# A new opening, maxima 42 items ahead and transposed a half later, and row sums inverted once on 128 partitions

## The chip, the core and the metric

The kernel runs on one core of a Trainium2 chip. The time is the device time of one execution in microseconds (us); three timed executions of the kernel before gave 4222.73 to 4227.74 us, with a median of 4225.1 us. The profile is of one more execution. The engines are PE (TensorE, matmuls), DVE (VectorE), ACT (ScalarE), POOL (GpSimd) and SP (SyncE, which only issues DMAs here).

## What is computed

The input x is 4 batches of 2048 tokens of 512 numbers, all in float32. It is normalized per token (layernorm without weights), and two things are added to x: attention with 16 heads of 32, whose queries and keys pass a filter in the frequency domain, and a layer of 8 experts that sends each token to the best one, at most 100 tokens to each.

```
xn = layernorm(x)
q, k, v = split(xn @ w_qkv)                       # 16 heads of 32
q, k = irfft(rfft(q) * mask), irfft(rfft(k) * mask)   # along the 32 of a head
out = softmax(q @ k.T / sqrt(32)) @ v             # 2048 x 2048 scores a head and batch
x + out @ w_out + b_out + experts(xn)
```

The filter is linear in a head's 32 numbers, so the kernel applies it once to the columns of w_qkv and not to q and k.

## The kernel before

**Tiles and loops.** Four heads are worked on together (HG = 4), so there are B * NG = 16 groups k of a batch and four heads, and each has NQ = 4 blocks of 512 queries: 64 blocks. A block goes over the 2048 keys in NT = 16 key tiles of 128. One key tile of a block is a *half*; two of them are a *window*. There are 1024 halves. In a half PE makes the scores of 128 keys by 512 queries for four heads (`scores`), ACT takes the exponentials into a tile `even` or `odd`, and PE multiplies the tile of the half before with v (`products`), which DVE adds up in `num`.

**Maxima.** The softmax subtracts each query's maximum, which must be known before a block's scores are made. So the scores are also made a first time, the other way round (queries on partitions), and DVE reduces them (`max_matmuls`, `max_reduce`, into `part`). An item of `stream` is 128 queries by 512 keys for two heads; 32 items make a block, and each half holds two items. The first MAX_AHEAD = 40 items are done in the opening, so a block's last item falls in half 11 of the block before the one before it is needed, 20 halves ahead. There DVE makes `neg` (`max_negate`), and at the end of the same half, or inside a projection of that half, PE transposes it (`max_turn`). ACT copies it (`max_store`), and at the head of the next window POOL splits it in three bfloat16 parts, which three SP DMAs `negm<-row` bring to four partitions (`max_split`). At a block's start PE puts them into the scores' banks (`shift`). After the first scores of a block, keys are held as differences of neighbours (`steps_of_keys`, by POOL), so that scores add up in PSUM from one key tile to the next.

**Row sums.** The exponentials of a block are added up pairwise: POOL issues a DMA that adds the odd tile to the even one (`even<-odd`, 1 MB, one a window), and POOL adds the result to that of the window before. Five halves into the next block PE sums the last tile over its 128 keys with a matrix of ones, and the four heads' sums stand on 32 equal partitions each (`close_steps`, `fold`; ACT copies them to `den`). DVE inverts `den` in eight pieces of 128x64, one a half in halves 6 to 13 (`invert`, into `factor`). At the head of half 14 POOL multiplies `num` with `factor` (`divide`, into `ot`). In halves 17 to 20 PE multiplies `ot` with w_out (`result`), and in half 21 POOL issues a DMA that adds the 1 MB to the output (`out_dram<-y`). The last block but one (of the 63 that are closed so) has other places, and the last block its own function.

**Order.** All engines work in the order in which the instructions are written out (`InOrder`). What is not the main line of a half is put into `agenda[half]` by `plan`: projections for the next group (pieces of 128 tokens, cost 1 each), token tiles of the next batch, the routing, loads. `spread` lays the pieces out so that PE's costs are even; key pieces may not come before a half that depends on MAX_AHEAD (`SPENT`), as the keys of the group are still needed by maxima. SP too issues in program order, but runs ahead of the others where a DMA has nothing to wait for.

**Opening.** SP loads the query and key columns of w_qkv (2 MB), the first batch of x (4 MB), and copies value columns. All four groups' weights are filtered (`filter_steps`: `turned` transposes on PE and copies on DVE, `filtered` multiplies on PE and copies on ACT), group 0's into `wg`, the others' through `wd` in DRAM. Then tokens are measured (DVE), scaled (POOL), normalized and transposed (`turn`). Projections of the first keys and queries go over 512 tokens at once. The first 40 items of maxima follow, one at a time, with turns and projections put in at written-out places (`ahead`).

Most instructions are issued by the helper in line 84 (`InOrder`), so that line says little in the profile; the names of tiles say more.

Of the kernel before, what the change touches and what calls it, by code (L numbers as in the profile page):

```python
# [39 lines left out]
PART = 64  # L40
WIN = 2
NW = NT // WIN
MAX_AHEAD = 40
# [3 lines left out]
def shape_constants():  # L47

    d = np.arange(DH)
    angle = 2.0 * np.pi * np.outer(np.arange(NF), d) / DH  # L50
    waves = np.concatenate([np.cos(angle), np.sin(angle)])

    waves[[NF, 2 * NF - 1]] = 0.0
    weight = np.full(NF, 2.0 / DH)
    weight[[0, NF - 1]] = 1.0 / DH
    weighted = waves * np.concatenate([weight, weight])[:, None]
    freq = np.stack([np.tile(weighted, (1, P // DH)), np.tile(waves, (1, P // DH))], axis=1)
    i = np.arange(P)
    eye = np.eye(P)
    upto = i[:, None] <= i[None, :]  # L60
    same_head = i[:, None] // DH == i[None, :] // DH
    square = np.stack([eye, upto, same_head], axis=1)
    falling = np.broadcast_to(E - np.arange(E), (P, E))
    token = np.arange(NT)[None, :] * P + i[:, None]
    return {
        "c_freq": freq.astype(np.float32),
        "c_square": square.astype(np.float32),
        "c_falling": np.ascontiguousarray(falling, dtype=np.float32),
        "c_token": token.astype(np.float32),
    }  # L70
# [33 lines left out]
def attention_and_top1_experts(ctx: ExitStack, tc: tile.TileContext, a: dict, out: bass.AP):  # L104
# [28 lines left out]

    mask = const.tile([2 * NF, 1], F32, name="mask")
# [5 lines left out]
    square = const.tile([P, 3, P], F32, name="square")  # L140
    nc.scalar.dma_start(out=square, in_=a["c_square"])
    ident, upto, same_head = (square[:, j, :] for j in range(3))
# [30 lines left out]
    wd = [dram1.tile([P, NR, 3, P], F32, name=f"wd{c}") for c in range(NG)]  # L173
    wg = {}
    raw = {}
    for s in range(2):
        both = probs(s == 1)
        for g in range(NR // 2):
            raw[s, g] = both[:, g]
            nc.sync.dma_start(out=raw[s, g], in_=w_qkv[:, 2 * g : 2 * g + 2, s * DM : (s + 1) * DM])  # L180
# [14 lines left out]
    def filter_steps(c):  # L195

        held = {}

        def turned(s):
            if s == 0:  # L200
                held["wt"] = probs(c % 2 == 1)
            pt = bank()
            for r in range(NR):
                on.tensor.transpose(
                    pt[:, r * P : (r + 1) * P], raw[s, r // 2][:, r % 2, c * P : (c + 1) * P], ident
                )
            on.vector.tensor_copy(held["wt"][:, s, 0, :], pt)

        def filtered(s):
            pw = bank()  # L210
            wt = held["wt"][:, s]
            for r in range(NR):
                at = slice(r * P, (r + 1) * P)
                on.tensor.matmul(pw[:, at], lhsT=wt[:, 0, at], rhs=filt, start=True, stop=True)
            done = pw.rearrange("p (r n) -> p r n", r=NR)
            if c == 0:
                on.scalar.copy(wg[0, s], done)
            else:
                on.scalar.copy(wt[:, 1, :], pw)
                nc.sync.dma_start(out=wd[c][:, :, s, :], in_=wt[:, 1, :].rearrange("p (r n) -> p r n", r=NR))  # L220

        return [lambda f=f, s=s: f(s) for s in range(2) for f in (turned, filtered)]
# [7 lines left out]
    def token_stage(b):  # L230
# [10 lines left out]
        def load_tile(i):  # L241
            n, t = divmod(i, TQ)
            if t == 0:
                held[n] = chunk("xs")
            on.sync.dma_start(out=held[n][:, t : t + 1, :], in_=x[b, n, :, t : t + 1, :])
# [163 lines left out]
    def load_qkv_weights(k, s):  # L409
        wg[k, s] = weights.tile([P, NR, P], F32, name=f"w{s}", bufs=1)  # L410
        on.sync.dma_start(out=wg[k, s], in_=wd[k % NG][:, :, s, :])
# [294 lines left out]
    def close_steps(k, n):  # L706
# [12 lines left out]

        def divide():  # L720
            held["ot"] = work.tile([P, QB], F32, tag="ot", name="ot", bufs=1)
            on.gpsimd.tensor_tensor(held["ot"], ended[k, n][0], held["factor"], ALU.mult)
# [15 lines left out]
        else:  # L738
            steps = [(5, 1, fold)] + [(6 + i, 0, invert, i) for i in range(QB // PART)]
# [20 lines left out]
    load, measure, scale, normalize, turn, first_route, first_sums, _ = token_stage(0)  # L760

    load(0)
# [3 lines left out]
    for s in range(3):  # L766
        wg[0, s] = weights.tile([P, NR, P], F32, name=f"w{s}", bufs=1)
    nc.sync.dma_start(out=wg[0, 2], in_=w_qkv[:, :, 2 * DM : 2 * DM + P])
    for c in range(1, NG):
        cols = slice(2 * DM + c * P, 2 * DM + (c + 1) * P)  # L770
        nc.sync.dma_start(out=wd[c][:, :, 2, :], in_=w_qkv[:, :, cols])
    filters = [filter_steps(c) for c in range(NG)]
    turned, filtered = ([f[2 * s + i] for f in filters for s in range(2)] for i in range(2))
    for i in range(2 * NG + 1):
        if i < 2 * NG:
            turned[i]()
        if i > 0:
            filtered[i - 1]()
        if 2 * NG - TQ <= i < 2 * NG:
            measure(i - 2 * NG + TQ)  # L780
    for s in range(3):
        nc.sync.dma_start(out=wd[0][:, :, s, :], in_=wg[0, s])
    first_projections = projections(0, TQ)
# [4 lines left out]
    for i in range(TQ):  # L788
        measure(TQ + i)
    scale(TQ, 2 * TQ, on.vector)  # L790
    for i in range(TQ, 2 * TQ):
        normalize(i)
        measure(TQ + i)
    first_projections[0]()
    scale(2 * TQ, 3 * TQ, on.vector)
    for i in range(2 * TQ, 3 * TQ):
        if i == 3 * TQ - 1:
            first_projections[1]()
        normalize(i)
        measure(TQ + i)  # L800
    scale(3 * TQ, NT, on.vector)
    falling = const.tile([P, E], F32, name="falling")
    nc.scalar.dma_start(out=falling, in_=a["c_falling"])
    token = const.tile([P, NT], F32, name="token")
    nc.scalar.dma_start(out=token, in_=a["c_token"])

    w_gate = const.tile([P, NR, DH], F32, name="w_gate")
    nc.gpsimd.memset(w_gate, 0.0)
    nc.scalar.dma_start(out=w_gate[:, :, 0:E], in_=a["L0_ffn_w_gate"].rearrange("(r p) e -> p r e", p=P))
    b_out = const.tile([P, DM], F32, name="b_out")  # L810
    nc.scalar.dma_start(out=b_out, in_=a["L0_attn_b_out"].partition_broadcast(P))


# [5 lines left out]
    for table in tables:  # L819
        nc.sync.dma_start(out=table.rearrange("(t p) c -> p t c", p=P), in_=nobody)  # L820

    load_out_weights(0)

    ahead = {6: first_projections[2], 14: first_projections[3], 22: first_projections[4]}
    ahead.update({28: first_projections[5], 33: first_projections[6]})
    for i, item in ((4, 1), (8, 9), (12, 17)):
        ahead.update({item + 2 * j: lambda i=i + 2 * j: (turn(i), turn(i + 1)) for j in range(2)})
    ahead.update({4: lambda: normalize(12), 5: lambda: normalize(13)})
    ahead.update({7: lambda: normalize(14), 8: lambda: normalize(15)})
    first_projections = projections(0)[7 * TQ :]  # L830
    on.sync = InOrder(tc, nc.sync)
    key_steps(0)
    closing = {}
    for i, item in enumerate(stream[:MAX_AHEAD]):
        if i == 30:
# [3 lines left out]
        half = next(turns), next(turns)  # L839
        max_matmuls(item, half)  # L840
        max_reduce(item, half, False)
        if i in ahead:
            ahead[i]()
        if i in (7, 15, 23):
            key_steps((i + 1) // 8)
        while full_blocks:
            closing[i + 2] = full_blocks.pop(0)
            max_negate(*closing[i + 2])
        if i in closing:
            negated.append(closing[i])  # L850
            max_store(max_turn(bank(), 0))
            max_split(*closing[i])
# [35 lines left out]
    def spread(steps, last):  # L888
# [4 lines left out]
        def places(level):  # L893
            half, done, found = base, costs[base], []
            for cost, first, _ in steps:
                while half < first or done + cost / 2 > level * (half - base + 1):
# [48 lines left out]
    def plan(k):  # L945
# [4 lines left out]
        def after_keys_are_spent():  # L950

            for i, place in enumerate([j for j, s in enumerate(kinds) if s == 1]):
                cost, _, step = steps[place]
                steps[place] = cost, start + SPENT + i // TQ * TQ, step

# [7 lines left out]
        steps, kinds = [], []  # L963
        if k == 0:
            done = spread([(1, 0, step) for step in first_projections], 15)
# [18 lines left out]
        if c == NG - 1:  # L984
# [14 lines left out]
            done = spread(steps, last)  # L999
# [6 lines left out]
        else:  # L1006
            steps = [(1, ready if k == 0 else start, step) for step in pieces]
            after_keys_are_spent()
            done = spread(steps, last)
# [37 lines left out]
    pairs, adds, splits = {}, {}, {}  # L1047
    left = None
    window = 0
    maxima = stream[MAX_AHEAD:]  # L1050
    for k in range(B * NG):
        for n in range(NQ):
            num = work.tile([P, QB], F32, tag="num", name="num")
            tiles = {}
            for w in range(NW):
# [9 lines left out]
                for j in (even, odd):  # L1065
# [16 lines left out]
                    while full_blocks:  # L1082
                        splits[window + 1] = full_blocks.pop(0)
                        max_negate(*splits[window + 1])
                        negated.append(splits[window + 1])
# [58 lines left out]
```

## Time and profile before

| | |
|---|---|
| median of three timed executions | 4225.1 us (4222.73 to 4227.74) |
| the profiled execution | 4220.07 us |
| its span, from the first to the last instruction | 4218.3 us |
| PE / DVE / ACT / POOL busy in it | 99% / 82% / 59% / 70% |
| mean granted clock of PE | 0.998 |
| first scores matmul (end of the opening) | 99.5 us |
| DMA engines' time taken by POOL's queue / SP's queue | 73.5% / 5.4% |

Busy shares are of the span. The chain is followed back from the last instruction, each time to what released it; its shares say on which engine the end depended. A group's line has the engine, the operation, output and inputs by name, the shape, the count, then busy us and the mean duration in ns, then the idle time of the engine just before. A line of the order of time has its start and duration in us, a count of merged instructions, and in brackets the idle time before it and what ended it. Weight loads (PEld) lie beside the matmuls. Matmuls are pipelined: the distance from start to start says more than a duration.

### The profile page before, as it was taken

How to read it: one execution, taken by the hardware profiler on the slowest of the kernel's cores; microseconds unless marked ns; L12 is line 12 of the kernel's file. 1: busy time of each engine (PE TensorE's matmuls, PEld its weight loads, DVE VectorE, ACT ScalarE, POOL GpSimd, SP SyncE). 2: the span in 40 equal slices, each digit the busy share in tenths (PEclk: the TensorE clock that was granted, in tenths of full speed). 3: DMA queues.
4: the chain of work that ended last, by engine and by line, in shares of the span. 5: the costliest groups of instructions: out<-in, count | busy, mean ns of one | idle time of the engine just before them, and what ended most of it. 6: DMA issues, size and time to landing. Idle time of an engine off the chain costs nothing.

```text
span 4218.3 us, 120261 instructions
## 1 busy us (share of the span) xinstructions
PE 4166.4 (99%) x52270; PEld 1837.7 (44%) x52270; DVE 3440.0 (82%) x4962; ACT 2489.1 (59%) x3411; POOL 2968.4 (70%) x2046
## 2 busy tenths in 40 slices
PE   8999999999999999999999999999999999999998
PEld 4444444444444444444444444444444443444432
DVE  6778888987788888897788888888778888788896
ACT  3555556666565556657565556566656555556665
POOL 1567776776876767776687766767668776677873
PEclk9999999999999999999999999999999999999999
DMA  4667778997788778899677787899877976778788
GB/s 121 144 139 154 155 159 163 220 197 151 139 158 161 155 156 164 187 199 193 132 158 157 156 161 150 162 199 203 169 148 146 183 158 134 148 160 165 156 170 178
DMA packets 183416, 685.93 MB, mean 163 GB/s; under 512 B 26902, under 2 KB 56760, under 8 KB 117608
## 3 DMA queue, kind: packets, MB, share of 16 engines
q0 software_dynamic: 110432, 605.83, 73.5%
q1 hardware_dynamic: 71280, 71.90, 5.4%
q8 instruction: 409, 6.70, 0.6%
q14 instruction: 119, 0.97, 0.1%
q10 hardware_dynamic: 1176, 0.52, 0.1%
HBM read 71.85 MB, written 88.96 MB: 38 GB/s over the span
## 4 chain that ended last, share of the span: by engine, by line
PE 93%; DVE 5%; DMA 1%; issue 1%; ACT 0%; POOL 0%; SPq 0%; ACTq 0%; POOLq 0%; DVEq 0%
PE array L84 93%; DVE part L84 3%; DVE num L84 1%; DVE factor L84 0%; DMA even<-odd 0%; ACT odd L84 0%; DVE stats L84 0%; DMA w<-wd 0%; ACT even L84 0%; DMA odd<-in_L_attn_w_qkv_dram 0%; DVE even L84 0%; POOL rstd L84 0%; DVE neg L84 0%; DMA mask<-_L_attn_mask_logits_dram 0%; DVE mv L84 0%
## 5 line engine op out<-in xcount | busy, mean ns | idle before, releaser
L84 DVE TENSOR_REDUCE part<-array 128x1 f32<-128x512 f32 (+1 forms) x3132 | 2483.3, 848 | 681.0 <-PE array L84 678.0
L84 POOL TENSOR_TENSOR even<-even 128x1024 f32<-128x1024 f32 x876 | 2123.6, 2528 | 410.5 <-DMA even<-odd 406.5
L84 PE MATMUL array<-keys,q 32*128 32x512 f32 x8192 | 2066.0, 614 | 7.9 <-DVE num L84 2.9
L84 PE MATMUL array<-q,steps_of_keys 32*128 32x512 f32 x8192 | 2030.7, 616 | 2.4 <-issue 2.1
L84 ACT ACTIVATE odd<-array 128x1024 f32<-128x1024 f32 x1024 | 996.0, 1021 | 483.3 <-PE array L84 413.4
L84 ACT ACTIVATE even<-array 128x1024 f32<-128x1024 f32 x1024 | 994.2, 1021 | 447.6 <-PE array L84 434.8
L84 PEld LDWEIGHTS array<-keys,q 32*128 32x128 f32 x8192 | 776.9, 184 | 565.8 <-DVE part L84 351.1
L84 PEld LDWEIGHTS array<-q,steps_of_keys 32*128 32x128 f32 x8192 | 691.9, 184 | 274.6 <-issue 250.8
L84 POOL DMA_DIRECT2D even<-odd x510 | 464.8, 911 | 394.9 <-ACT odd L84 346.6
L84 DVE TENSOR_TENSOR num<-num,array 128x512 f32<-128x512 f32 x960 | 650.5, 678 | 23.5 <-PE array L84 23.4
L84 PEld LDWEIGHTS array<-xnT,w 128*32 128x32 f32 x15808 | 443.3, 110 | 264.0 <-DVE part L84 172.3
L84 PE MATMUL array<-even,v 128*32 128x512 f32 x4096 | 545.5, 605 | 1.0 <-DVE part L84 1.0
L84 PE MATMUL array<-odd,v 128*32 128x512 f32 x4096 | 545.9, 605 | 0.0
L84 PE MATMUL array<-xnT,w 128*32 128x128 f32 (+1 forms) x15808 | 525.2, 277 | 1.5 <-ACT xnT L84 0.7
L84 PEld LDWEIGHTS array<-w,xnT 128*32 128x32 f32 x8192 | 230.4, 110 | 146.8 <-DVE part L84 106.6
L84 DVE RECIPROCAL factor<-den 128x64 f32<-128x64 f32 x504 | 274.4, 545 | 0.0
L84 PE MATMUL array<-wo,ot 128*32 128x512 f32 x2048 | 267.0, 594 | 5.0 <-POOL ot L84 5.0
L84 PE MATMUL array<-w,xnT 128*32 128x128 f32 x8192 | 269.4, 273 | 1.3 <-DMA w<-wd 1.1
L84 PEld LDWEIGHTS array<-even,v 128*32 128x32 f32 x4096 | 80.6, 108 | 390.1 <-DVE part L84 381.2
L84 PEld LDWEIGHTS array<-odd,v 128*32 128x32 f32 x4096 | 80.8, 108 | 388.4 <-DVE part L84 379.9
L84 POOL DMA_DIRECT2D out_dram<-y x63 | 86.5, 1373 | 202.8 <-ACT y L84 125.6
L84 ACT COPY q<-array 128x128 f32<-128x128 f32 (+1 forms) x250 | 66.9, 268 | 186.1 <-PE array L84 182.3
(129 smaller groups left out, 1478.9 us busy)
## 6 DMA issues: line engine op xcount, KB each, us to landing
even<-odd POOLq DMA_DIRECT2D x510, 1024.0 KB, 8.4
out_dram<-y POOLq DMA_DIRECT2D x63, 1024.0 KB, 9.8
xs<-in_L_attn_x_dram SPq DMA_DIRECT2D x96, 256.0 KB
out_dram<-in_L_attn_x_dram SPq DMA_DIRECT2D x16, 1024.0 KB
w<-wd SPq DMA_DIRECT2D x45, 256.0 KB
wo<-in_L_attn_w_out_dram SPq DMA_DIRECT2D x16, 256.0 KB
negm<-row SPq DMA_DIRECT2D x192, 4.0 KB
xs<-in_L_attn_x_dram SPq DMA_DIRECT2D x2, 1024.0 KB
```

What stands on the lines that cost most here:

```text
L84: done = act(*args, **kwargs)
```

## The change

**Row sums.** For 62 of the 63 blocks, the eight reciprocals are replaced. In half 6 an SP DMA takes one partition of `den` for each head (4 x 512) and lays it out as 128 partitions of 16, in the first 16 columns of `factor` (`apart`). In half 9 DVE inverts these in place (`invert_all`). In half 10 an SP DMA writes them to DRAM (`lay_down`), and in half 12 four SP DMAs read each head's 512 numbers back onto 32 partitions (`to_rows`). The division stays at the head of half 14. The last block but one keeps its eight reciprocals.

**Maxima.** MAX_AHEAD is 42, so a block's last item falls in half 10. `max_negate` stays there, but the block is entered in `negated` only in the next half, so that PE transposes in half 11; `max_split` stays at the head of the next window.

**Opening.** The constant matrices come in one DMA on SP's queue, ahead of all. Of w_qkv the first 128 query and key columns are loaded first, then the first four token tiles in two DMAs, then the remaining columns and the rest of x. Group 0's weights are filtered first, group 1's around the first token tiles, groups 2 and 3 beside the maxima. Projections are pieces of 128 tokens throughout. 42 items of maxima are done in 21 pairs: the matmuls of both items, then both reductions, then the steps in `beside[p]`. Value weights are read from w_qkv directly and no longer copied to DRAM. The four tables are cleared by a DMA with a contiguous run for each partition, beside the last pairs.

**Plan.** `SPENT` follows MAX_AHEAD and comes one half earlier; `spread` is given the latest half of each key piece and does not pass it.

```diff
-MAX_AHEAD = 40
+MAX_AHEAD = 42
+APART = HG * QB // P
...
+    square = const.tile([P, 3 * P + E + NT], F32, name="square")
+    nc.sync.dma_start(out=square, in_=a["c_square"])
...
     for s in range(2):
-        both = probs(s == 1)
-        for g in range(NR // 2):
-            raw[s, g] = both[:, g]
-            nc.sync.dma_start(out=raw[s, g], in_=w_qkv[:, 2 * g : 2 * g + 2, s * DM : (s + 1) * DM])
+        raw[s] = probs(s == 1).rearrange("p g r n -> p (g r) n")
+        nc.sync.dma_start(out=raw[s][:, :, 0:P], in_=w_qkv[:, :, s * DM : s * DM + P])
...
+        def apart():
+            on.sync.dma_start(out=held["factor"][:, 0:APART], in_=held["den"][0::DH, :])
+
+        def invert_all():
+            at = held["factor"][:, 0:APART]
+            on.vector.reciprocal(at, at)
+
+        def lay_down():
+            held["all"] = scratch.tile([P, APART], F32, name="inverses")
+            on.sync.dma_start(out=held["all"], in_=held["factor"][:, 0:APART])
+
+        def to_rows():
+            for h in range(HG):
+                row = held["all"][DH * h : DH * (h + 1), :].rearrange("r c -> (r c)")
+                on.sync.dma_start(out=held["factor"][DH * h : DH * (h + 1), :], in_=row.partition_broadcast(DH))
...
-            steps = [(5, 1, fold)] + [(6 + i, 0, invert, i) for i in range(QB // PART)]
+            steps = [(5, 1, fold), (6, 0, apart), (9, 0, invert_all), (10, 0, lay_down), (12, 0, to_rows)]
             first = 17
...
+    for step in (*turned0, *filtered0):
+        step()
+    for i in range(TQ):
+        measure(i)
+    for step in turned1:
+        step()
     scale(0, TQ, on.vector)
     for i in range(TQ):
         normalize(i, fast=True)
         turn(i)
-    for i in range(TQ):
-        measure(TQ + i)
-    scale(TQ, 2 * TQ, on.vector)
+    for step in filtered1:
+        step()
+    for i in range(TQ, 2 * TQ):
+        measure(i)
+    scale(TQ, 2 * TQ)
+    for i in range(TQ + 1):
+        project_first(i)
...
+    for p, pieces in enumerate(((5,), (6, 8), (7, 9), (10, 11), (12,), (13,), (14,), (15,), (16,), (17,), (18,), (19,))):
+        beside[p] += [lambda i=i: project_first(i) for i in pieces]
+    for i in range(TQ):
+        beside[i].insert(0, lambda i=i: turn(TQ + i))
+        beside[3 * TQ + i].append(lambda i=i: project_first(5 * TQ + i))
+        beside[4 * TQ + i].append(lambda i=i: project_first(6 * TQ + i))
+    for n in (1, 2):
+        for i in range(TQ // 2):
+            for t in (2 * i, 2 * i + 1):
+                beside[TQ * n + i].insert(t % 2, lambda t=t, n=n: turn((n + 1) * TQ + t))
+    for i in range(TQ):
+        beside[i // 2].append(lambda i=i: measure(3 * TQ + i))
...
+    for p, step in zip((6, 7, 8, 9, 10, 11, 12, 13), (*turned2, *filtered2, *turned3, *filtered3)):
+        beside[p].append(step)
...
-        half = next(turns), next(turns)
-        max_matmuls(item, half)
-        max_reduce(item, half, False)
-        if i in ahead:
-            ahead[i]()
+        both = [(item, (next(turns), next(turns))) for item in stream[2 * p : 2 * p + 2]]
+        for item, half in both:
+            max_matmuls(item, half)
+        for item, half in both:
+            max_reduce(item, half, False)
...
+                latest[place] = start + SPENT + i // TQ * TQ + 3 * TQ - 1
...
-                    while full_blocks:
-                        splits[window + 1] = full_blocks.pop(0)
-                        max_negate(*splits[window + 1])
-                        negated.append(splits[window + 1])
+                    negated.extend(fresh)
+                    if negated:
+                        splits[window + 1] = negated[0]
+                    fresh = [full_blocks.pop(0) for _ in range(len(full_blocks))]
+                    for filled in fresh:
+                        max_negate(*filled)
```

## The prediction

> **What bounds the kernel now.** I read the page's busy shares and chain first, then the waits, then the order of time inside single steps. A step is one key tile of one block: 4 maxima matmuls for a later block, 4 scores matmuls, 4 products and what the agenda adds. The source calls it a half.
>
> ```profile
> PE 4166.4 (99%) x52270; PEld 1837.7 (44%) x52270; DVE 3440.0 (82%) x4962; ACT 2489.1 (59%) x3411; POOL 2968.4 (70%) x2046
> PE 93%; DVE 5%; DMA 1%; issue 1%; ACT 0%; POOL 0%; SPq 0%; ACTq 0%; POOLq 0%; DVEq 0%
> L84 DVE RECIPROCAL factor<-den 128x64 f32<-128x64 f32 x504 | 274.4, 545 | 0.0
> PE array L84 <- DVE neg L84: 13.0, 15, 0.9
> ```
>
> PE is the bound nearly everywhere, so 274.4 us of reciprocals on DVE are not 274.4 us to win. I cut the trace at the first scores matmul of every half: 1024 halves from 99.5 us on. With one projection piece a half takes 3.80 us, the same in 165 halves that hold a reciprocal as in 63 that hold none. With two pieces and two reciprocals 45 halves take 4.67 us, as those without do. Only empty halves (no projection, result or fold) follow DVE. One of them in order of time, and below it the transposition of the negated maxima, once a block in its half 11, first in an empty half, then behind a projection:
>
> ```profile
> 4070.94 0.70 PE L84 MATMUL array<-keys,q 32*128 32x512 f32 x2
> 4071.41 0.67 DVE L84 TENSOR_TENSOR num<-num,array 128x512 f32<-128x512 f32 x1
> 4072.00 0.54 DVE L84 RECIPROCAL factor<-den 128x64 f32<-128x64 f32 x1
> 4072.46 2.41 DVE L84 TENSOR_REDUCE part<-array 128x1 f32<-128x512 f32 x4
> 4074.33 0.70 PE L84 MATMUL array<-keys,q 32*128 32x512 f32 x2
> ...
> 796.92 1.06 PE L84 MATMUL array<-even,v 128*32 128x512 f32 x8
> 798.61 0.22 DVE L84 TENSOR_REDUCE neg<-part 128x16 f32<-128x64 f32 x1
> 798.88 0.39 PE L84 MATMUL array<-square,neg 128*16 128x128 f32 x2 [0.89 <-DVE neg L84]
> 799.20 0.70 PE L84 MATMUL array<-keys,q 32*128 32x512 f32 x2
> ...
> 734.83 1.06 PE L84 MATMUL array<-xnT,w 128*32 128x128 f32 x32
> 735.63 0.22 DVE L84 TENSOR_REDUCE neg<-part 128x16 f32<-128x64 f32 x1
> 735.91 0.39 PE L84 MATMUL array<-square,neg 128*16 128x128 f32 x2
> ```
>
> In the first stretch DVE has no gap: 3.39 us a half, of which the reciprocal takes 0.46 (4072.00 to 4072.46). In the second PE stands 0.89 us until DVE has made neg. In the third a piece (0.99 us from start to next start) is followed 1.08 us later: PE loses 0.09. The transposition itself holds PE for 0.32 us (798.88 to 799.20).
>
> The opening is the third place; from the chain, and from the order of time on PE and DVE:
>
> ```profile
> 24.76 1.91 DVE xs L84 x4
> 92.10 7.00 DVE part L84 x8
> 99.14 50.17 PE array L84 x762
> ...
> 48.01 3.64 PE L84 MATMUL array<-xnT,w 128*32 128x512 f32 x32
> 52.85 9.26 DVE L84 TENSOR_REDUCE part<-array 128x2 f32<-128x1024 f32 x8 [2.44 <-PE array L84]
> ```
>
> PE starts the first maxima at 40.2 and the first half at 99.5. Between, DVE reduces 40 items at 1.17 us (9.26 / 8; 46.6 us) and stands 10.1 us waiting for PE, mostly 2.4 us behind each projection of 512 tokens.
>
> **Part 1, row sums.** 62 of 63 blocks lose 8 reciprocals of 0.545 us and gain one of 128x16 (0.25 us by the routing's row of that shape), six SP DMAs and two more waits. Where PE sets the half this is worth 0. It counts in 23 empty halves at 3.39: the 16 empty ones with maxima but no reciprocal take 3.02 to 3.25; I take 3.10, 23 x 0.29 = 6.7 us (ends: 0.14 each, and the whole 0.46). Nine halves that also turn a token tile take 4.52 to 4.76 against 4.28: 2.5 us. Six with two pieces exceed 4.67: 2.2 us. Sum 11.4 (ends 6 and 15).
>
> The price is waiting. *apart* sits in half 6, but SP issues it as soon as ACT has made den; invert_all stands in DVE's order where the fourth reciprocal starts now, 13.6 to 21.0 us behind den; the small end is in blocks of empty halves, which lose three reciprocals ahead of it: 12.7. If it lands later, DVE stops, and with it the maxima, the products' sums and so PE. The nearest row is a load w<-wd, alone on SP's queue: 512 packets, 32 on each of 16 engines. By the trace's packets its first starts 1.2 to 5.4 us after the issue, and its last ends 2.7 to 12.8 us after; the one issued nearest behind an output DMA (3688.2, as apart will be) ends after 11.1. While the accumulating DMAs run, SP's queue and theirs alternate packet by packet, 26 against 26 in a microsecond. So I take about 11 us: it lands 1.7 us early or more, cost 0 (the far end is rival A).
>
> lay_down waits for DVE at half 9 and has until half 12; behind it are only loads due halves later and negm, due at half 16. to_rows (4 issues, by negm's 0.53 us each 2.1 us) follows the three negm in SP's order, and 8 packets an engine land 2 to 7 us later: about half 14 to 15, where POOL divides. POOL may stand 0 to 4 us there, with the next accumulating DMA behind it. I cost that at nothing: POOL is idle 30%; an odd tile is written again 10 us (median) after its DMA has landed, 4.4 us at least for the DMA in question; ot is read in half 17. Without that cover each microsecond is one of ACT's and PE's.
>
> How apart is split is not in the trace, but negm is: 4 partitions written, 16 data packets and 4 of four bytes, so four engines. The Trainium skill (DMA: Bandwidth & Descriptors, "Why a DMA increments its semaphore by 16 and not by 1") says that a DMA takes the largest number of engines up to 16 that divides both sides' slowest dimension, and negm agrees. By this rule apart (4 partitions read, 128 written) has four engines with 32 packets of 64 bytes each, not 16 with 8. Spread over 16, apart would land some 5 us earlier and rival A would fall away; the sum would be the same.
>
> **Part 2, transposed a half later.** neg is then a half old when PE wants it. 10 empty halves of 4.21 (blocks 6, 10, 18 and on) become max(PE, DVE) = 3.2 us: PE's products to 797.80 plus 0.32 give 3.13, DVE 3.10. That is 10.1 us; four of 4.50 with a reciprocal in them (53, 60, 61, 62) also go to 3.2: 5.2 us. 47 behind a projection lose 0.09: 4.2 us. neg now runs in half 10, empty in four blocks: 0.6 back. Sum 18.9 (ends 11 and 22). The split and the negm DMAs stay in window 6, so their readers see no change.
>
> **Part 3, opening.** The filter's first two turns end near 10.2, their products by 14 at the present rows (1.92 each; the square's transfer and the first columns are under 1 MB and 312 GB/s are shown, so they land before). The second group's two copies (0.69) end at 16.8 on DVE, and normalizing four tiles (1.91) at 19. Turning ends 20.6, filter products 22.1, five pieces of 0.99 at the clock of 0.83 shown there by 28.2, ACT's copy 0.7: first maxima about 29, 11 us earlier. Then DVE needs 42 x 1.17 + four measures of 0.80 + neg = 52.5 us. PE needs per pair 1.06 plus what stands beside it (turn 0.55, piece 0.99, filter step 0.6 or 1.06); where that exceeds DVE's 2.33 (pairs 2 to 13: 1.3, 1.3, 0.8, 0.8, 0.3, 0.3, 1.9, 1.9, 0.3, 0.3, 0.8, 0.8) DVE waits, 11 us. 29.5 + 63.5 gives a first half at 93 to 94, against 99.5: 6 us. Ends: no waiting, 82; a start 2 us later and 4 us of copies not hidden, 99.5. Everything that SP gains here is issued before a main wait. Two items fewer in the loop empty one half of maxima at the end: 0.3. The plan of pieces moves four into empty halves, under 1 us.
>
> **Sum.** 11.4 + 18.9 + 6 + 0.3 = 36.6. The profiled execution took 4220.07 us (span 4218.3), 5.0 under the median of 4225.1. 4220.07 - 36.6 = 4183.5; on the median's side 4188.5. Changes under 0.2% (8.5 us) cannot be told from none.
>
> **Rivals.**
> A (slower): apart lands behind DVE's arrival. For: the DMA engines are taken without a gap in most blocks just then; with the load's 32 packets an engine, 33 turns at 1.6 a microsecond after a start of 5.3 are 26 us. Against: the output DMA's smaller packets give faster turns, and loads of that count have never taken over 12.8. It decides from 0.6 us late in every block (36.6 / 62). At 2 us late: 62 x 2 = 124, so 4312. Chance 0.12.
> B: the opening gains nothing, as PE's pieces and copies merely replace DVE's waiting: 4194. For: 11 us of new waiting against 10.1. Chance 0.15.
> C: DVE stays the bound of empty halves by its reductions and half 11 keeps half its wait: 4204. Against: DVE is shown idle in the half behind. Chance 0.10.
> D: the change does little, since POOL's wait for factor delays accumulating DMAs and eats the gain: 4220. Chance 0.08.
> Mine: 0.55, with its own range 4174 to 4203. The range for 8 in 10 leaves out A and half of D: 4172 to 4216. Faster 0.55 + 0.15 + 0.10 + 0.02 = 0.82, same 0.05, slower 0.13.
>
> **What would show it.** Right: the wait for neg gone from PE, half 11 at 3.2 or about 4.1; empty halves near 3.10; first half near 93; POOL waiting for a DMA ahead of ot. Wrong: DVE waiting for den's transfer ahead of the 128x16 reciprocal (A), or the loop's start near 99 (B).

## The result, and the profile after

The changed kernel is slower: 4249.1 us in the median (4239.2 to 4254.2), against 4225.1; the ratio is 1.0052, with an interval of 1.0036 to 1.0069. I had forecast 4188.5. The profiled execution is the fastest of these, 4239.23 us with a span of 4237.4, so the traces, whose spans differ by 19.1 us, show less of the loss than the medians, 24.0.

From the page of the changed kernel the busy shares and the chain by engine (the chain can be followed back only to 3280 us, so its shares add up to 23% of the span and can't be set beside those of before); then, from its groups by line, the division and the two kinds of reciprocals; then, from its waits (engine and tile, what it waited for, us in all, times, longest):

```profile
PE 4176.9 (99%) x52846; PEld 1855.8 (44%) x52846; DVE 3227.2 (76%) x4518; ACT 2491.3 (59%) x3436; POOL 2965.4 (70%) x2052
...
PE 18%; DMA 2%; DVE 1%; issue 1%; POOL 1%; ACT 0%; SPq 0%; POOLq 0%; ACTq 0%; DVEq 0%
```

```profile
L83 POOL TENSOR_TENSOR ot<-num,factor 128x512 f32<-128x512 f32 x63 | 81.4, 1291 | 224.2 <-DMA factor<-inverses 116.9 <-PE array L83 55.6 <-DVE part L83 25.0
L83 DVE RECIPROCAL factor<-factor 128x16 f32<-128x16 f32 x62 | 15.3, 246 | 4.8 <-issue 4.7
L83 DVE RECIPROCAL factor<-den 128x64 f32<-128x64 f32 x8 | 3.8, 520 | 0.0
```

```profile
POOL even L83 <- DMA even<-odd: 517.5, 198, 7.9
POOL ot L83 <- DMA factor<-inverses: 116.9, 35, 4.5
ACT even L83 <- POOL even L83: 66.5, 30, 4.1
ACT odd L83 <- DMA even<-odd: 18.3, 10, 5.0
PEld array L83 <- POOL ot L83: 16.4, 13, 3.2
PE array L83 <- POOL ot L83: 6.1, 6, 1.7
PEld array L83 <- DVE neg L83: 1.9, 2, 1.1
```

What the change was to do, it did. DVE has 212.8 us less to do, its reciprocals 19.1 us instead of 274.4, and the wait for neg is gone. What is new is idle time of POOL ahead of the division: 224.2 us in all (before 31.3), 212.2 of them in the 62 changed blocks (before 23.3), 3.45 in the median block. The profile lays it on several releasers, the signal that came last; that it is the rows in all of them, two of the runs below show, where it is gone. Four of these waits in the kernel before:

```profile
POOL even L84 <- DMA even<-odd: 412.2, 185, 7.7
ACT even L84 <- POOL even L84: 3.1, 3, 1.5
ACT odd L84 <- DMA even<-odd: 1.0, 1, 1.0
PEld array L84 <- DVE neg L84: 40.5, 63, 1.8
```

So the stall of POOL runs on: to the addition of the tiles, from there to ACT, which may not write an even tile again until POOL has read it (3.1 us before, 66.5 now), and from ACT to PE. In the halves: the first one starts at 93.86 us (before 99.52), 5.7 us gained; the 1024 halves take 4143.5 us (before 4118.8), 24.7 us lost.

Block 27 shows it in order of time, POOL, SP and ACT of the changed kernel (start, duration, in brackets the idle time before and what ended it):

```profile
1881.58 11.61 SPq L83 DMA_DIRECT2D negm<-row  x3
1893.29 3.29 SPq L83 DMA_DIRECT2D factor<-inverses  x4
...
1889.79 1.26 POOL L83 TENSOR_TENSOR steps_of_keys<-keys 128x512 f32<-128x512 f32 x1
1891.02 0.42 POOL L83 TENSOR_TENSOR rest<-rest,row 16x128 f32<-16x128 f32 x1
...
1892.59 0.88 POOL L83 DMA_DIRECT2D even<-odd  x1
1893.19 4.97 POOL L83 TENSOR_TENSOR even<-even 128x1024 f32<-128x1024 f32 x2
1901.66 1.27 POOL L83 TENSOR_TENSOR ot<-num,factor 128x512 f32<-128x512 f32 x1 [3.49 <-PE array L83]
1902.88 0.88 POOL L83 DMA_DIRECT2D even<-odd  x1
1903.47 4.99 POOL L83 TENSOR_TENSOR even<-even 128x1024 f32<-128x1024 f32 x2
...
1908.49 1.94 ACT L83 ACTIVATE even<-array 128x1024 f32<-128x1024 f32 x2 [3.07 <-POOL even L83]
```

Half 12 starts at 1881.0 and half 14 at 1888.8. POOL is behind: it splits the maxima only from 1891.02 on, as it must first make the keys' differences. SP waits with the negm DMAs for the splits, and the rows stand behind negm: they are issued at 1893.29 and after. POOL has done its addition at 1898.16 and stands 3.5 us for the rows. The division starts 12.8 us into half 14, the accumulating DMA and the next addition after it, ACT stands 3.07 us, and half 18 (the halves are counted on into the next block) takes 6.97 us instead of 4.55. Half 19 takes 5.42 instead of 3.78; from 1912.1 to 1915.5 the granted clock is 0.50. The same POOL before, where nothing keeps the division:

```profile
1893.53 4.98 POOL L84 TENSOR_TENSOR even<-even 128x1024 f32<-128x1024 f32 x2
1898.16 1.58 POOL L84 TENSOR_TENSOR ot<-num,factor 128x512 f32<-128x512 f32 x1
1899.37 1.20 POOL L84 DMA_DIRECT2D even<-odd  x1
1901.72 4.67 POOL L84 TENSOR_TENSOR even<-even 128x1024 f32<-128x1024 f32 x2 [1.15 <-DMA even<-odd]
```

### The profile page after: what moved, and what is told of

It reads as the page before. It is cut to its first block, busy times and chain, and to the rows that moved or that the text cites. A ratio compares the mean times of both kernels' runs of the same rounds, so it can differ in the third digit from the quotient of the medians.

```text
span 4237.4 us, 121737 instructions
## 1 busy us (share of the span) xinstructions
PE 4176.9 (99%) x52846; PEld 1855.8 (44%) x52846; DVE 3227.2 (76%) x4518; ACT 2491.3 (59%) x3436; POOL 2965.4 (70%) x2052
## 5 line engine op out<-in xcount | busy, mean ns | idle before, releaser
L83 POOL DMA_DIRECT2D even<-odd x510 | 484.1, 951 | 239.5 <-ACT odd L83 212.3
L83 PEld LDWEIGHTS array<-xnT,w 128*32 128x32 f32 x16384 | 457.8, 110 | 256.3 <-DVE part L83 175.2
L83 PE MATMUL array<-xnT,w 128*32 128x128 f32 x16384 | 525.9, 273 | 1.1 <-DVE part L83 0.6
L83 POOL TENSOR_TENSOR ot<-num,factor 128x512 f32<-128x512 f32 x63 | 81.4, 1291 | 224.2 <-DMA factor<-inverses 116.9
L83 ACT COPY q<-array 128x128 f32<-128x128 f32 x256 | 67.9, 265 | 181.6 <-PE array L83 179.4
L83 ACT COPY v<-array 128x128 f32<-128x128 f32 x256 | 68.0, 266 | 181.4 <-PE array L83 179.0
```

The lines of the kernel that those rows point to most:

```text
L83: done = act(*args, **kwargs)
```

## The experiments

Ratios are to the kernel before on the same chip. Several versions are compared by their ratios, 0.001 of which is 4.2 us.

**Which part loses.** The changed kernel with the old reciprocals, and the kernel before with nothing but the new row sums.

```
- steps = [(5, 1, fold), (6, 0, apart), (9, 0, invert_all), (10, 0, lay_down), (12, 0, to_rows)]
+ steps = [(5, 1, fold)] + [(6 + i, 0, invert, i) for i in range(QB // PART)]
```

> The changed kernel with the eight reciprocals of 128x64 put back; the opening, the 42 items and the later transposition stay. Its profile gives three theories. W: POOL stands at its division until the row sums have come back (3.45 us in the median block, 212 us in all), and this delays the accumulating DMAs, which come back as waits of ACT and PE. X: the six small transfers a block take the DMA engines from the accumulating DMAs, whoever waits. Y: the row sums are harmless, and the loop lost its time to the new plan of pieces and the 42 items. By W and X the loss goes with the row sums: before (4225) less 6 for the opening, less 15 for half 11, plus 5 for key pieces that now end just in time: 4209, between 4203 and 4215. By Y it stays: 4249 or, as 11 us of reciprocals come back, 4260.

> The kernel before with the new row sums alone (the transfers, one inversion, the division at the head of half 14); opening, 40 items and transposition as before. By W and X it is slower than both kernels: 4225 plus some 45 of waits less 11 of reciprocals, 4250 to 4265. By Y it is faster than before: 4214. What I had forecast of this part alone was 4225 - 11 = 4214 too.

Measured: 4203.7 us, 0.9950 (0.9937 to 0.9964), without them; 4271.2 us, 1.0112 (1.0096 to 1.0127), with them alone. In the trace of the second POOL stands 204 us before the division. Its waits:

```profile
POOL ot L85 <- DMA factor<-inverses: 104.5, 31, 5.3
POOL ot L85 <- PE array L85: 72.5, 23, 4.8
ACT even L85 <- POOL even L85: 57.7, 31, 3.8
ACT odd L85 <- DMA even<-odd: 26.2, 15, 3.5
```

The row sums lose all of it, and the rest of the change gains half a per cent. Y, by which the row sums were harmless, falls. Between W (POOL's wait) and X (the transfers themselves) these two don't tell.

**Wait or transfers.** Two versions that keep every transfer. In the first POOL multiplies with den and leaves the inverses unused; in the second the rows are issued in half 11, ahead of negm.

```
- on.gpsimd.tensor_tensor(held["ot"], ended[k, n][0], held["factor"], ALU.mult)
+ on.gpsimd.tensor_tensor(held["ot"], ended[k, n][0], held["den"], ALU.mult)
```

```
- (10, 0, lay_down), (12, 0, to_rows)]
+ (10, 0, lay_down), (11, 0, to_rows)]
```

> The changed kernel, all transfers in place, but POOL multiplies with den and not with factor, so nothing waits for the last transfers (the result is num times the sum and not num over the sum; the work of every engine and queue is the same). By W the time falls to what I had forecast less the just-in-time pieces, 4195 to 4208, and POOL's division starts within 1 us of half 14. By X it stays near 4249, as the transfers are the same. By Y it stays too.

> The changed kernel with to_rows in half 11 and not in half 12, and so ahead of the three negm DMAs in SP's order and not behind them. By W the last transfer lands 4 to 8 us sooner, POOL's wait at the division falls from 212 us to under 60 in all, and the time to 4200 to 4215. By X nothing moves but the order: 4245 to 4252. A risk of its own: negm's first DMA is queued behind to_rows (3.4 us of issues); it is due at half 16 and should not show.

Measured: 4198.7 us, 0.9943 (0.9930 to 0.9957), and 4203.7 us, 0.9954 (0.9940 to 0.9967). POOL's idle time before the division is 0.16 and 0.15 us, for all 62 blocks together, and the version with earlier rows shows these waits:

```profile
POOL even L83 <- DMA even<-odd: 433.5, 201, 7.9
ACT even L83 <- POOL even L83: 8.5, 9, 2.4
DVE factor L83 <- DMA factor<-den: 5.2, 1, 5.2
ACT odd L83 <- DMA even<-odd: 2.7, 1, 2.7
```

The transfers are all there and the loss is gone: X falls, W holds. In the second version to_rows go out 4.6 us before half 12 (median), in the changed kernel 3.8 us after its start, 12.2 at most.

**The order on POOL, or the late ot.** The division put behind the accumulating DMA and the addition, the rows as late as in the changed kernel:

```
- heads[end + half].append(divide)
+ (agenda if half == 14 else heads)[end + half].append(divide)
```

> The changed kernel with POOL's division no longer at the head of half 14 but at that half's end, behind the issue of the accumulating DMA and POOL's addition; to_rows stays in half 12, so the rows land as late as before. Theory W (the division's wait holds back what stands behind it on POOL): the DMA and the addition go out on time again, the division starts some 5.5 us into half 14 with the rows mostly there (they land 4.7 us into it in the median, 13.3 at most), and nearly all of the loss is gone: 4204 to 4212. Rival V: it is the late ot itself that costs, through PE's products with w_out in half 17: ot is then as late as now or later, so the time stays at 4240 to 4250 or rises.

Measured: 4211.1 us, 0.9977 (0.9968 to 0.9986). The division now starts 8.2 us into half 14 (median), later than the 4.7 of the changed kernel, yet three quarters of the loss are gone. V, by which the late ot itself costs, explains at most the rest, 0.0023 or 10 us over the version with earlier rows, and the waits of PE for ot have grown, from 12.8 us there to 32.2:

```profile
PEld array L83 <- POOL ot L83: 20.6, 11, 4.6
PE array L83 <- POOL ot L83: 11.6, 6, 3.7
POOL ot L83 <- DMA factor<-inverses: 2.8, 1, 2.8
```

**How much hold costs.** POOL's wait in the changed kernel is 2 to 5 us in nearly every block, but the traces, set beside each other block by block, show loss only in some. So I held POOL by a fixed amount, with nothing to wait for (on the version with earlier rows):

```
+ for _ in range(4):      # 7 in the other
      on.gpsimd.tensor_tensor(held["ot"], ended[k, n][0], held["factor"], ALU.mult)
```

> The version with to_rows in half 11 (nothing waits at the division), and POOL multiplies num with factor four times into the same tile: it is held 3 x 1.27 = 3.8 us longer at the head of half 14, in every block by the same amount, about as long as it stands there in the changed kernel (3.45 us in the median). Theory H: a hold of that size in every block is what costs; then as in the changed kernel, 4240 to 4250. Theory L: a hold of 4 us is covered, as my forecast had it, and what costs are the blocks in which to_rows stand behind negm, negm behind POOL's late splits, and POOL's division behind to_rows, so that POOL starts the division 10 us or more late; in the trace of the changed kernel 37 blocks whose division starts less than 6 us late lose nothing and 9 above 10 us lose 2.7 us each. Then POOL, held by a fixed amount, is late by little more than that: 4204 to 4214.

> As with four times, but seven: POOL is held 6 x 1.27 = 7.6 us longer in every block, more than ever in one wait of the changed kernel. By the trace of the changed kernel a division that ends 6 to 10 us late costs a block 0.3 to 0.6 us and one over 10 us late 2.7: theory L 62 blocks x 0.5 to 2.7 us on 4204, so 4235 to 4370, with ACT waiting for POOL's addition on the even tile. Theory H: twice the hold, at least twice the loss of 40 us: 4285 or more, and the version with four times at 4245. If POOL's idle time covers even this: 4204 to 4214.

Measured: 4273.7 us, 1.0119 (1.0102 to 1.0136), and 4468.9 us, 1.0586 (1.0568 to 1.0603). For four times both theories fail: L by 60 us, for a fixed hold is not covered, and H by 24. For seven times L's upper end is passed by 99 us, while H's open bound holds. The traces tell why. Sorted by where the last multiplication ends in half 14, with the time of the 16 halves from half 12 on against the version with earlier rows (blocks, us lost a block):

| end of the division in half 14 | changed kernel | four times | seven times |
|---|---|---|---|
| before 6 us | 30, -0.12 | 20, -0.10 | 0 |
| 6 to 8 us | 11, 0.17 | 14, 0.26 | 1, 0.02 |
| 8 to 10 us | 7, 0.95 | 10, 1.47 | 5, 3.0 |
| over 10 us | 14, 2.4 | 18, 2.8 | 56, 4.3 |

The loss goes with how late the division ends, and with the accumulating DMA and the addition behind it. Up to some 8 us it is 0.3 us a block or less in all three, over 10 us 2.4 to 4.3. The end alone does not set it: between 8 and 10 us the five blocks of seven times lose 3.0, the seven of the changed kernel 0.95. An ordinary block gets there with 7.6 us of hold, not with 3.8; a block whose POOL is late anyway gets there with 3.8, and there L had left out that POOL's own lateness adds to the hold.

The granted clock has a part in the dearest blocks. Within the halves counted here it is 0.50 for stretches of 3.4 to 6.8 us in four blocks of the changed kernel, all in its last row; in each, one begins within 1.5 us of the end of a stall of PE of 1.2 to 1.7 us. With seven divisions there are such stretches in 23 blocks, with four in six, with earlier rows in one, before and with the old reciprocals in none. Half of the stretches' length, 9.6 us in the changed kernel and 68.6 with seven divisions, is at most what they cost, an estimate, of the 38.7 and 255.2 us that the two lose in these halves.

**Which blocks.** The changed kernel again, with the old reciprocals in the 21 blocks whose division started more than 7 us into half 14 (a block has here the number of the one that is divided; its half 14 lies in the next):

```
+ LATE = (3, 9, 10, 11, 15, 16, 25, 26, 30, 31, 32, 41, 42, 46, 47, 48, 49, 50, 59, 60, 61)
...
+ elif k * NQ + n in LATE:
+     steps = [(5, 1, fold)] + [(6 + i, 0, invert, i) for i in range(QB // PART)]
+     first = 17
```

> The changed kernel, to_rows in half 12 and the division at the head of half 14, but the 21 blocks (of 62) in whose trace POOL starts the division more than 7 us into half 14 keep their eight reciprocals; in the other 41 POOL stands before the division as in the changed kernel (3.4 us in the median, some 135 us in all). Theory T (the hold costs nothing until the division is some 8 us late, and POOL must already be late, or the rows be held back by its late splits, to get there): by the trace the 21 blocks hold 37.6 us of loss against the version with reciprocals everywhere, the other 41 hold 0.2; so 4249 - 38 to 45 = 4204 to 4211. Theory H (each hold costs about alike): 21 of 62 parts of 45 us are gone, 4234.

Measured: 4204.7 us (4202.5 to 4215.5), 0.9965 (0.9953 to 0.9976), in T's bounds and 29 us below H. POOL still stands 137.4 us before the division, in 41 blocks:

```profile
POOL ot L84 <- DMA factor<-inverses: 62.4, 19, 4.5
POOL ot L84 <- PE array L84: 36.7, 11, 4.7
ACT even L84 <- POOL even L84: 36.6, 29, 2.5
```

Of the 35.3 us that the halves of the changed kernel lose against the version with reciprocals everywhere, 28.3 go with a third of the blocks. T's 0.2 us for the rest was too little: 7.0 us stay, and 12 blocks still start the division over 7 us late, 10.6 at most. Eight of the 12 have the old reciprocals and do not stand for rows; what makes them late this run does not show.

**The other parts.** The maxima transposed in the same half again, the latest halves of the key pieces one sooner, both on the version with earlier rows, and on top of the sooner keys the last group by reciprocals:

```
- negated.extend(fresh)
- if negated:
-     splits[window + 1] = negated[0]
- fresh = [full_blocks.pop(0) for _ in range(len(full_blocks))]
- for filled in fresh:
-     max_negate(*filled)
+ while full_blocks:
+     splits[window + 1] = full_blocks.pop(0)
+     max_negate(*splits[window + 1])
+     negated.append(splits[window + 1])
```

> The version with to_rows in half 11, and the maxima negated and transposed in the same half again (now half 10). Prices a half later by itself, with nothing waiting at the division. My forecast's term was 18.9 us; the trace of the changed kernel shows half 11 at 4.00 us behind a projection (before 4.21) and at 3.63 us when empty (before 4.21), 15.0 us less in all. If that is the whole of it: 4203.7 + 13 to 16 = 4217 to 4220, with the wait of PE for neg back on some 60 blocks. If the 42 items alone made the difference (the last item in half 10 instead of 11): 4204, and half 10 no longer than now.

```
- latest[place] = start + SPENT + i // TQ * TQ + 3 * TQ - 1
+ latest[place] = start + SPENT + i // TQ * TQ + 3 * TQ - 2
```

> The version with to_rows in half 11, and the latest half of each key piece one half sooner (start + 53 instead of start + 54 for the first four). In ten blocks of the changed kernel half 6 takes 5.13 us instead of 4.67, because the next maxima need the keys of a piece in the half just before and wait for ACT's copy of them. If that wait is all: 4203.7 - 4.6 = 4199, and half 6 back at 4.67. If the pieces only move the wait to half 5: 4204.

```
+ elif k == B * NG - 1:
+     steps = [(5, 1, fold)] + [(6 + i, 0, invert, i) for i in range(QB // PART)]
+     first = 17
```

> As the version with key pieces one half sooner, and the last group's two blocks (60 and 61) keep their eight reciprocals. In the version with to_rows in half 11 one half of block 60 takes 5.8 us too long, because DVE stands before the 128x16 reciprocal for the transfer of den; in those halves PE has nothing else to do, so a block is short and the transfer late. If that is the only place: some 5 us less than with the row sums in all blocks, 4194. If the late transfer is luck and moves from block to block: the same as without, 4199.

Measured: 4215.9 us, 0.9990 (0.9981 to 1.0000), for the same half; the difference from 0.9954 is 0.0036, 15 us (8 to 22 by the two intervals), and the wait for neg is back (24.5 us of PE's weight loads on 62 blocks, before 40.5 on 63). So the half later is worth some 15 us by the medians, and the 42 items alone are not it. The trace, of this run's slowest execution, has 25.1 us between the totals of the halves.

The sooner keys give 4199.6 us, 0.9948 (0.9935 to 0.9962), which the interval doesn't tell from 0.9954. The trace does: half 6 of the ten blocks falls to 3.10 us, 20.3 in all, half 5 and half 7 rise by 18.8 and 5.0, and all halves together take 4107.0 us, as before the edit (4107.4). The work only moved. With the last group by reciprocals it is 4201.3 us, 0.9954 (0.9940 to 0.9967), no gain over the sooner keys, although the trace's halves take 5.0 us less than theirs.

## Why the prediction was wrong, point by point

**The step that failed** is the one on to_rows: "POOL may stand 0 to 4 us there, with the next accumulating DMA behind it. I cost that at nothing". In the traces this term is the whole loss: 35.3 us in the halves. The size of the wait was right (3.45 us in the median; its DMAs take 3.35 us to issue, where I had 2.1, and the division starts 5.3 us after the last). The cover was not, for three reasons that the traces show:

- I reckoned with a POOL that is on time, from its 30% of idle time. In the trace of before the division starts more than 3 us into half 14 in 10 blocks, at most 6.9. To such a POOL the wait is added. After the change 21 blocks start it more than 7 us late, at most 13.3.
- I saw that to_rows "follows the three negm in SP's order" and took negm's time as fixed. But negm waits for POOL's splits. In before they start over 3 us into half 12 in 9 blocks, in the changed kernel in 24, with the rows ahead of negm in 12. A late POOL makes negm late, negm the rows, and the rows POOL: so read, the two queues wait for each other in turn, and lateness grows.
- I priced the odd tile (4.4 us of room at least) and ot, and neither gave way first. What did was the even tile, which ACT waits to write until POOL has added it: 66.5 us, against 18.3 for the odd one.

Rival D named this mechanism, with 0.08 and a price of 4220, as if it could take the gain and no more. I had the point from which it decides in my own hands: some 4 us of cover beside 3 to 7 us of lateness that were in the trace of before.

**Row sums, 11.4 us.** About 5. Between the versions with the old reciprocals and with earlier rows, the empty halves 8 and 10 shorten by 0.29 as I had it, the empty halves 7 and 9 from 3.39 to 3.26 and 3.25 only: 4.1 us in 21 halves, and 0.6 in the halves 11 of blocks 53 and 61. The nine token-turn halves stay at 4.52 to 4.69, but for one that falls from 4.76 to 4.52, and those with two pieces at 4.67; their excess was not the reciprocals', and 4.7 us of my sum were laid on the wrong cause. In the version with earlier rows one late transfer of den (half 10 of block 60 takes 8.89 us, in the changed kernel 3.10) eats even this: 0.9954 against 0.9950 with the reciprocals, which the intervals don't tell apart.

**Rival A** did not come: apart's last packet ends 11.1 us after the issue (median; I had about 11), and DVE stood for it in 2 of 62 blocks, 4.8 us in all. In 33 blocks its packets can be seen alone, 128 of 64 bytes and 4 of four bytes, so four engines, as the rule of the Trainium skill that I had weighed (DMA: Bandwidth & Descriptors, "Why a DMA increments its semaphore by 16 and not by 1") gives it. But 17.6 at most is beyond my 12.8 from the loads.

**Transposed a half later, 18.9 us.** The sum was right, its parts were not. The 64 halves 11 take 256.7 us in all, before 271.7, which is 15.0 less; but the last block's, which holds no transposition, went from 2.92 to 6.89, and the other 63 take 19.0 less. The run with the same half says 15, within its intervals. Behind a projection half 11 went from 4.21 to 4.00 rather than 4.12, more than I had; empty ones from 4.21 to 3.63, not 3.2, less. There PE waits again, now for the last reduction, after the transposition has been done at 786.96. From the order of time of the changed kernel:

```profile
786.96 0.38 PE L83 MATMUL array<-square,neg 128*16 128x128 f32 x2
...
787.78 0.70 PE L83 MATMUL array<-keys,q 32*128 32x512 f32 x2 [0.44 <-DVE part L83]
```

This is a part of rival C, 0.43 in ten halves; what those behind projections gain beyond the forecast makes up for it.

**Opening, 6 us.** 5.7: the first half starts at 93.86, forecast 93 to 94, and the parts hold too. The first maxima start at 27.7 (I had 29), DVE's first reduction at 28.92 (29.5); from there DVE is busy 52.6 us (52.5) and waits 11.7 (11). In the other runs with this opening the first half starts at 92.0 to 94.4. Rival B did not come.

**Plan of pieces, "under 1 us".** It costs some 4 us. In ten blocks the last two key pieces now stand in half 6, the latest that they may, and the next maxima need their keys: 5.13 us instead of 4.67, which this line of the changed kernel begins (order of time; PE waits for ACT's copy):

```profile
581.10 0.70 PE L83 MATMUL array<-keys,q 32*128 32x512 f32 x2 [0.39 <-ACT keys L83]
```

The sum by the traces, the halves without the new row sums taken from the run with the old reciprocals: opening -5.7; half 11 of the first 63 blocks -18.4, halves 6 and 7 of the ten blocks +4.2, the last block +4.7, all else -1.1, together -10.6 (4118.8 to 4108.2); the row sums with their wait +35.3 (4108.2 to 4143.5). That is +19.0, and the spans differ by 19.1.

## What to carry to other kernels

A wait on a queue that works in order is not covered by the queue's idle share: take, block by block, how late the queue already is, add the wait, and compare with the room of everything behind it. Where the transfer that ends the wait stands on another queue behind something that the first queue must make, the two delay each other; put it ahead, or put the waiting instruction behind the work that others need. The versions with the rows one half earlier, or with the old reciprocals, are the better ones here: 4200 to 4204 us, half a per cent below the kernel before. By the run with the old reciprocals the opening, the later transposition and the plan give that alone; what the new row sums add without their wait, these runs can't tell.

## What the runs showed of the hardware

Small transfers on SP's queue take long where the accumulating DMAs run: the 8 KB of apart have their first packet 5.0 us after the issue and their last end 11.1 after it (medians of 62; the quickest end 1.6 after). The Trainium skill (DMA: Bandwidth & Descriptors, "Anatomy of one DMA — SWDGE (gpsimd) path") fits 2.0 us plus the bytes at 436 GB/s, for DMAs that GpSimd issues; worked out for 8 KB, an estimate, that is 2.0 us, and the runs here show over five times as much for one from SP beside other traffic.

Four small DMAs cost their queue, too: the issues of to_rows take 3.35 us (0.57 for one in the median, 2.91 at most), during which SP issues nothing else.
